# A four-layer graph network on one core: VectorE's order in two attention layers taken from the source, and a layer's second pass cut in two

## The chip, the core and the metric

The kernel runs on one core of a Trainium2 chip. A core has five engines that each work through their own list of instructions: TensorE (PE in the profile; its weight loads are shown as PEld), VectorE (DVE), ScalarE (ACT), GpSimd (POOL) and SyncE (SP), which here only issues loads. An engine takes its instructions strictly in the order of its list, and they wait for each other across engines through semaphores. The metric is the device time of one execution in microseconds.

## What is computed

4096 nodes with 64 features each pass through four layers, each followed by a residual and a layer norm, over one dense 4096 x 4096 matrix of zeros and ones (64 MB in float32, read once per layer from DRAM):

```python
x = _layernorm(x + _L0_gnn_ref(x, adj, L0_gnn_W, L0_gnn_b), axis=-1)       # mean over neighbours, linear, relu
x = _layernorm(x + _L1_gnn_ref(x, adj, L1_gnn_r, L1_gnn_w_att, ...), axis=-1)  # hyperbolic attention
x = _layernorm(x + _L2_gnn_ref(x, adj, L2_gnn_weight, L2_gnn_bias), axis=-1)   # weights 2**-(rank among neighbours)
x = _layernorm(x + _L3_gnn_ref(x, adj, L3_gnn_att_w, ...), axis=-1)        # hyperbolic attention
```

Layers 1 and 3 do the same work: for every pair (i, j) the sigmoid of left[i] + right[j], times the edge, times a distance factor, and the sum over j of that times a vector of node j. Then each node is moved by that sum on the hyperbolic ball, which is a long chain of small formulas with one value per node (norms, reciprocal square roots, a tanh).

## The kernel before

**Tiling.** The receiving nodes are cut into 4 groups of 1024 (`GROUPS` = 3, 2, 1, 0, in that order), the sending nodes into 32 blocks of 128, taken from 31 down to 0, two at a time (a step `g`, 16 steps per group). One load (`load`, L655) brings 128 x 2 x 1024 edges, 1 MB, into one of six buffers.

**Attention (layers 1 and 3).** `attend` does one group. For each of the two blocks `k` of a step, TensorE puts six matmuls of 512 columns into a tile `z` of PSUM (L935, L938, L941; two such tiles exist), ScalarE computes a sigmoid (L943) and a square of z (L946), and VectorE multiplies (L949). After both blocks VectorE combines 2048 columns (L951), and TensorE adds the result into `acc` with four float32 matmuls (L955). So a step holds three large VectorE instructions: L949, L949, L951.

**The rest of a layer** is written as Python generators that are put into two queues and advanced while the large loops are traced: `tick(n)` advances them n times, and a generator says with `yield k` how many ticks to wait before its next piece. `need(tag)` ticks until a piece is done. In a step of attention there are three ticks' places: after each L949 and after the matmuls L955; `rate` ticks at each. The generators that matter here:

- `move` (L966): for a group whose sums are complete, four transposes, a reduce, then the chain of the hyperbolic step: 128x8 instructions (one value per node) on VectorE, six 128x512 ones (L988, L991, L997, L999, L1068, L1071), two products on GpSimd (L992, L1067), a square and a tanh on ScalarE. It holds three `rsqrt` (L669), each a chain of ten 128x8 instructions in which every one reads the one before. Its tiles (u, w_att, k, ...) exist once, so that one group's move can't pass another's.
- `linear` (L1073): the layer 2 linear of a moved group, in halves.
- `norm_rows` (L761) and `prepare` (L782): layer norm, and everything that the next attention needs of a group: 128x8 chains, six 128x512 instructions, casts and four copies on ScalarE, 32 transposes on TensorE, and two logarithms for which ScalarE loads another table.
- `spread_left` (L899): the left values of a group, spread over partitions (L904, L910).

How long a generator waits is set by `soon`, `near` and `after`, which look at `place[0]`, the stage: 0 for layer 0, 1 for layer 1, 2 for layer 2, 3 for layer 3.

**Who sets the order.** The framework's scheduler orders the instructions of each engine by its own estimate of when they can start, unless an engine is named in `tc.manual_schedule(engines=...)`: there it keeps the order in which the source issued them. Before, layers 0 and 2 fix TensorE and ScalarE (`FIXED`); in both attention layers every engine's order is the scheduler's. What came out for VectorE in attention: nearly everywhere one small instruction between two large ones, so three per step.

**Layer 2** makes two passes (L1316 on), each over two groups at once: for each block and group four matmuls into the group's `z` (L1340), an exponential of 1024 columns on ScalarE (L1349) and, one turn later, four matmuls into the group's `acc` (L1356). VectorE only checks every second load (L741, 128x2048). When a pass ends, both its groups go on to `end_2` and then to `norm_rows` and `prepare` of layer 3.

**The tail.** After the last step of layer 3 the last group's `move` remains, and the store of its rows.

Of the kernel before, what the change touches and what calls it, by code (L numbers as in the profile page):

```python
# [19 lines left out]
P = 128  # L20
# [38 lines left out]
def gnn_stack_kernel(  # L59
# [509 lines left out]
    def stream(fits):  # L569

        with ExitStack() as st:
# [46 lines left out]
            def soon():  # L618


                return 0 if place[0] in (0, 2) else 1

            def after(small):


                each = {0: 1.6, 2: 6.0}.get(place[0])
                return 1 if each is None else 1 + int(small / each)
# [41 lines left out]
            def rsqrt(a, name):  # L669

                n = a.shape[1]
                r, t = nums(name, n), nums("rs_t", n)
                V.tensor_scalar(
                    r.bitcast(I32), a.bitcast(I32), -0.5, float(0x5F3759DF), ALU.mult, ALU.add
                )
                for _ in range(3):
                    V.tensor_mul(t, r, r)
                    V.scalar_tensor_tensor(t, t, -0.5, a, ALU.mult, ALU.mult)
                    V.scalar_tensor_tensor(r, t, 1.5, r, ALU.add, ALU.mult)
                return r  # L680
# [64 lines left out]
            def curved(c, name, least):  # L745
# [7 lines left out]
                V.tensor_copy(rsc, rsqrt(c, "rsc"))  # L753
# [7 lines left out]
            def norm_rows(layer, s, v, x2_to):  # L761
# [7 lines left out]
                yield soon()  # L769
                yield soon()  # L770
# [3 lines left out]
                r = rsqrt(m, "n_r")  # L774
# [6 lines left out]
            def prepare(layer, s, att, b_att, curve, least, good, small):  # L781
# [7 lines left out]
                V.reciprocal(rbg, bg)  # L789

# [6 lines left out]
                def second():  # L797
# [16 lines left out]
                    V.tensor_sub(ys[:, :, D : 2 * D], y, ys[:, :, :D])  # L814
# [4 lines left out]
                    yield 1  # L819
                    V.tensor_add(w, xg, over(g))  # L820
                    yield 1
                    V.tensor_mul(xe[:, at, :], w, over(m))

# [3 lines left out]
                    rt = rsqrt(q1, "rt")  # L827
# [34 lines left out]
                    yield 1  # L862
# [109 lines left out]
            def move(layer, s, sums, curve):  # L972
# [14 lines left out]
                yield near()  # L987
# [7 lines left out]
                yield near()  # L995
                yield soon()
# [9 lines left out]
                V.scalar_tensor_tensor(t2, d, -2.0, kx, ALU.mult, ALU.add)  # L1006
                V.tensor_mul(t2, t2, k)
# [7 lines left out]
                V.scalar_tensor_tensor(un, t2, root, rsqrt(t2, "r_t2"), ALU.mult, ALU.mult)  # L1015
# [5 lines left out]
                yield near()  # L1021
# [11 lines left out]
                V.tensor_add(den, den, xy)  # L1033
                V.tensor_sub(p, y2, p)
# [10 lines left out]
                V.scalar_tensor_tensor(w2, qd, 2.0, px, ALU.mult, ALU.add)  # L1045
                V.tensor_mul(t, t, uu)
# [5 lines left out]
                n = rsqrt(t, "n")  # L1052
# [10 lines left out]
                r = rsqrt(w2, "n")  # L1063
# [5 lines left out]
                yield soon()  # L1069
                yield soon()  # L1070
# [3 lines left out]
            def linear(layer, s, weights, finish):  # L1074

                for h in range(2):
# [19 lines left out]
                    finish(slice(s * WB + h * SB, s * WB + (h + 1) * SB), t)  # L1096
# [3 lines left out]
            def supports(at, t):  # L1100

                nc.scalar.activation(halves[:, at, :D], t, AF.Copy, scale=SUP)
                V.scalar_tensor_tensor(
                    halves[:, at, D:], t, SUP, halves[:, at, :D], ALU.mult, ALU.subtract
                )
# [21 lines left out]
            with ExitStack() as lp:  # L1127
# [45 lines left out]
                def own_part(at, t):  # L1173

                    V.tensor_add(xw[:, at, :], t, b0_sb[:, None, :].to_broadcast([P, SB, D]))

                def end_0(s, tops):
# [3 lines left out]
                    for top, low in tops:  # L1181
# [6 lines left out]
                        ts.append(t)  # L1188
                    for h, t in enumerate(ts):
# [6 lines left out]
                    held.clear()  # L1196
                    V.tensor_scalar(z, z, 0.0, None, ALU.max)
                    sq, n2 = grp("sq"), nums("n2")
                    nc.gpsimd.tensor_mul(sq, z, z)
                    yield 1  # L1200
                    V.tensor_reduce(n2, sq, AX.X, ALU.add)
                    V.tensor_scalar(n2, n2, 1e-24, None, ALU.max)
                    n = rsqrt(n2, "n")
# [9 lines left out]
                with tc.manual_schedule(engines=FIXED):  # L1213
                    for s in GROUPS:
# [42 lines left out]
                        if s > 0:  # L1257
                            own_of = linear(0, s - 1, w0_sb[:D, :], own_part)
                            later(in_turn((0, s - 1), own_of))

# [20 lines left out]


            attention(1, curve1, (2, 1, 1, 1), lambda s: linear(2, s, w2_sb, supports))


            place[0] = 2

            def end_2(s, sums):
# [4 lines left out]
                yield 1  # L1293
# [15 lines left out]
            lag = []  # L1309

            def flush():

                while lag:
                    lag.pop(0)()

            with tc.manual_schedule(engines=FIXED):  # L1316
                for n in range(0, NW, 2):
                    two = GROUPS[n : n + 2]
                    zs = [ps.tile([P, WW], F32, name="z") for _ in two]

                    accs = [[] for _ in two]
                    behind = [None, None]
                    for g in reversed(range(NB // 2)):
                        edges = []
                        for s in two:
                            a, edge = load(s, g)
                            if g % 2 == 1:
                                junk = sb.tile([P, 2, WW], F32, name="t").bitcast(BF16)
                                check(s, g, a, junk[:, 0, :].rearrange("p (b i) -> p b i", b=2))
                            edges.append(edge)  # L1330
                        need((2, 2 * g // WB))
                        for k in (1, 0):
                            j = 2 * g + k
                            for i, edge in enumerate(edges):
                                z, acc = zs[i], accs[i]
                                here = edge[:, k * WW : (k + 1) * WW]
                                for lhs, rhs in ((pass_by, behind[i]), (enter, here)):
                                    for h in range(0, WW, W):
                                        if rhs is not None:
                                            nc.tensor.matmul(  # L1340
                                                z[:, h : h + W], lhs, rhs[:, h : h + W],
                                                start=j == BLOCKS[0], stop=True,
                                                skip_group_check=True,
                                            )
                                behind[i] = here
                                flush()

                                w = sb.tile([P, 2, WW], F32, name="sq").bitcast(BF16)[:, 0, :WW]
                                nc.scalar.activation(w, z, AF.Exp, bias=at_edge, scale=-LN2)  # L1349

                                def add(acc=acc, j=j, w=w):
                                    if not acc:
                                        acc.append(ps.tile([P, W], F32, name="acc"))
                                    for part in range(2):
                                        for h in range(2):
                                            nc.tensor.matmul(  # L1356
                                                acc[0][h * D : (h + 1) * D, :],
                                                halves[:, j, part * D : (part + 1) * D],
                                                w[:, h * W : (h + 1) * W],
                                                start=j == BLOCKS[0] and part == 0,  # L1360
                                                stop=j == BLOCKS[-1] and part == 1,
                                            )

# [102 lines left out]
```

## Time and profile before

Three executions took 1150.9 to 1157.15 us, median 1155.24. The profiled one took 1151.7 us, of which its span on the core is 1150.0 us; the other 1.7 us lie around it. By stages, from the trace (busy us of each engine in the stretch, the granted TensorE clock as a share of full speed, and what the DMA queues moved):

| stage | from, to (us) | length | PE | DVE | ACT | clock | GB/s |
|---|---|---|---|---|---|---|---|
| layer 0 | 0 to 192.7 | 192.7 | 167.7 | 147.2 | 38.0 | 0.96 | 386 |
| layer 1, attention | 192.7 to 537.6 | 344.9 | 320.5 | 328.7 | 300.0 | 0.98 | 196 |
| layer 2 | 537.6 to 764.7 | 227.1 | 212.3 | 123.5 | 167.8 | 0.99 | 284 |
| layer 3, attention | 764.7 to 1114.9 | 350.2 | 316.6 | 337.2 | 304.2 | 0.98 | 184 |
| tail | 1114.9 to 1150.0 | 35.1 | 2.9 | 24.2 | 2.2 | 0.58 | 18 |

In lines of a timeline the columns are: start and duration in us, engine, line of the source, operation, tile written <- tiles read, shapes, count, and in brackets the engine's idle time before it and what ended it. [...]what an instruction costs is the distance from its start to the next one's.

### The profile page before, as it was taken

The page shows a single profiled execution, that of the slowest core. Times are in us where ns is not written, and L with a number is a line of the kernel's source. Part 1 is how long each engine was busy: PE and PEld are TensorE (multiplying, and loading weights), DVE is VectorE, ACT ScalarE, POOL GpSimd, SP SyncE. Part 2 cuts the span into 40 slices and gives each one's busy share as a digit, 9 for nine tenths or more (in the row PEclk, how much of TensorE's full clock was granted, in tenths as well). Part 3 has the DMA queues.
Part 4 walks back from the last instruction along what each step waited for, and adds up shares of the span by engine and source line. Part 5 has one row for each costly group of instructions (what it writes and reads, how often), then busy time and mean ns, then how long its engine had stood idle before and what let it go on. Part 6 is the DMA issues. An engine that isn't in the chain of part 4 may idle for free.

```text
span 1150.0 us, 13516 instructions
## 1 busy us (share of the span) xinstructions
PE 1019.8 (89%) x4917; PEld 389.6 (34%) x4917; DVE 960.8 (84%) x1901; ACT 812.2 (71%) x823; POOL 60.9 (5%) x97
## 2 busy tenths in 40 slices
PE   6889997899899999988999997998788999899970
PEld 3445554233333333332333232332323333233220
DVE  7587888989999899989773584249988999999996
ACT  0003215899889799976767688777997999889860
POOL 0020120000000000000000020001100000000001
PEclk9998998999999999999999999999998999999995
DMA  9999898546456455643988886695354655555400
GB/s 352 421 385 412 358 390 337 199 158 217 180 214 220 156 214 215 220 160 141 323 300 310 314 308 255 227 358 193 110 183 155 223 213 215 210 211 212 154 0 22
DMA packets 38418, 271.57 MB, mean 236 GB/s; under 512 B 4550, under 2 KB 4550, under 8 KB 5574
## 3 DMA queue, kind: packets, MB, share of 16 engines
q1 hardware_dynamic: 37440, 269.50, 63.0%
q10 hardware_dynamic: 902, 1.12, 0.3%
q8 instruction: 40, 0.66, 0.2%
q14 instruction: 36, 0.29, 0.1%
HBM read 269.55 MB, written 1.05 MB: 235 GB/s over the span
## 4 chain that ended last, share of the span: by engine, by line
DVE 54%; PE 30%; ACT 6%; DMA 5%; issue 2%; POOL 2%; ACTq 0%; POOLq 0%; SPq 0%; DVEq 0%
DVE t L951 21%; DVE t L949 21%; PE z L1340 9%; PE acc L1356 5%; PE acc L1229 5%; DMA edges<-in_adj_dram 5%; PE acc L955 3%; ACT sq L946 2%; ACT sq L1349 1%; PE aux L1092 1%; PE z L935 1%; PE aux L842 1%; ACT sig L943 1%; PE z L938 1%; DVE junk L741 1%
## 5 line engine op out<-in xcount | busy, mean ns | idle before, releaser
L943 ACT ACTIVATE sig<-left_b,right 128x1024 f32<-128x1024 f32 x256 | 293.8, 1149 | 44.8 <-DVE t L949 33.7
L949 DVE SCALAR_TENSOR_TENSOR t<-z,sig 128x1024 f32<-128x1024 f32 x256 | 309.8, 1215 | 15.5 <-ACT sq L946 14.6
L946 ACT ACTIVATE sq<-z,turn 128x1024 f32<-128x1024 f32 x256 | 281.4, 1105 | 30.2 <-PE z L941 27.9
L951 DVE SCALAR_TENSOR_TENSOR t<-sq,t 128x2048 f32<-128x2048 f32 x128 | 292.9, 2288 | 0.7
L955 PE MATMUL acc<-t,xe 128*64 128x512 f32 x1024 | 260.3, 622 | 33.5 <-DVE t L951 30.0
L935 PE MATMUL z<-edges,two_i 128*128 128x512 bf16 x512 | 202.7, 396 | 20.5 <-DVE t L949 20.3
L941 PE MATMUL z<-dst,src 74*128 74x512 f16 x512 | 196.2, 383 | 0.0
L938 PE MATMUL z<-lo_hi,hi_lo 128*128 128x512 f16 x512 | 195.4, 382 | 0.0
L1349 ACT ACTIVATE sq<-z,at_edge 128x1024 bf16<-128x1024 f32 x128 | 141.8, 1113 | 57.0 <-PE z L1340 56.1
L955 PEld LDWEIGHTS acc<-t,xe 128*64 128x64 f32 x1024 | 64.2, 139 | 171.3 <-DVE t L951 89.3
L741 DVE SCALAR_TENSOR_TENSOR t<-edges 128x2048 bf16<-128x2048 f32 x32 | 73.7, 2312 | 47.1 <-DMA edges<-in_adj_dram 46.2
L1229 PE MATMUL acc<-edges,first 128*128 128x512 bf16 x256 | 82.5, 404 | 19.4 <-DMA edges<-in_adj_dram 19.4
L935 PEld LDWEIGHTS <-two_i 128*128 128x128 bf16 x512 | 50.5, 99 | 141.6 <-issue 97.7
L1356 PE MATMUL acc<-sq,halves 128*64 128x512 bf16 x512 | 80.1, 393 | 16.8 <-ACT sq L1349 16.1
L1229 PE MATMUL acc<-edges,third 128*65 128x512 bf16 x256 | 81.8, 402 | 0.0
L741 DVE SCALAR_TENSOR_TENSOR junk<-edges 128x2048 bf16<-128x2048 f32 x32 | 73.1, 2285 | 7.8 <-DMA edges<-in_adj_dram 7.5
L1340 PE MATMUL z<-edges,enter 128*128 128x512 bf16 x256 | 78.9, 390 | 0.0
L1340 PE MATMUL z<-edges,pass_by 128*128 128x512 bf16 x248 | 77.8, 394 | 0.0
L938 PEld LDWEIGHTS <-hi_lo 128*128 128x128 f16 x512 | 50.5, 99 | 69.4 <-issue 25.8
L941 PEld LDWEIGHTS <-src 74*128 74x128 f16 x512 | 49.6, 97 | 69.3 <-issue 5.1
L1356 PEld LDWEIGHTS <-halves 128*64 128x64 f16 x512 | 19.2, 108 | 73.9 <-issue 73.8
L1229 PEld LDWEIGHTS <-first 128*128 128x128 bf16 x256 | 24.4, 100 | 48.1 <-issue 21.0
(260 smaller groups left out, 758.9 us busy)
## 6 DMA issues: line engine op xcount, KB each, us to landing
edges<-in_adj_dram SPq DMA_DIRECT2D x256, 1024.0 KB, 5.6
x<-in_x_dram SPq DMA_DIRECT2D x4, 256.0 KB
out_dram<-x ACTq DMA_DIRECT2D x4, 256.0 KB, 4.2
w_sb<-in_L_gnn_W_dram ACTq DMA_DIRECT2D x1, 32.0 KB, 4.7
given<-in_L_gnn_b_dram ACTq DMA_DIRECT2D x1, 0.2 KB
given<-in_L_gnn_bias_dram ACTq DMA_DIRECT2D x1, 0.2 KB
given<-in_L_gnn_b_att_dram ACTq DMA_DIRECT2D x1, 0.0 KB
given<-in_L_gnn_att_b_dram ACTq DMA_DIRECT2D x1, 0.0 KB
```

The costliest lines, as they stand in the source:

```text
L741: V.scalar_tensor_tensor(junk, a, 0.0, a, ALU.not_equal, ALU.not_equal, accum_out=odd[:, n : n + 1])
L935: nc.tensor.matmul(half, two_i, edge[:, at : at + W], start=True, stop=False)
L938: nc.tensor.matmul(half, hi_lo[:, of], lo_hi[:, to], start=False, stop=False)
L941: nc.tensor.matmul(half, src[:, of], dst[:, to], start=False, stop=True)
L943: nc.scalar.activation(sig, left_b, AF.Sigmoid, bias=right[:, j : j + 1])
L946: nc.scalar.activation(sq[:, k], zp, AF.Square, bias=turn, scale=-1.0 / UNIT)
L949: V.scalar_tensor_tensor(t[:, k], zp, 0.0, sig, ALU.max, ALU.mult)
L951: V.scalar_tensor_tensor(t, sq, HIGH**2, t, ALU.add, ALU.mult)
L955: nc.tensor.matmul(acc[h * D : (h + 1) * D, :], xe[:, j, :], t[:, k, h * W : (h + 1) * W], start=j == BLOCKS[0], stop=j == BLOCKS[-1],)
L1229: nc.tensor.matmul(accs[h][:m], lhs[:, j, :], edge[:, at : at + W], start=j == BLOCKS[0], stop=j == BLOCKS[-1],)
L1340: nc.tensor.matmul(z[:, h : h + W], lhs, rhs[:, h : h + W], start=j == BLOCKS[0], stop=True, skip_group_check=True,)
L1356: nc.tensor.matmul(acc[0][h * D : (h + 1) * D, :], halves[:, j, part * D : (part + 1) * D], w[:, h * W : (h + 1) * W], start=j == BLOCKS[0 ...
```

## The change

Five things change; in the changed file the lines below L617 move down by 3 to 16, and further in layer 2.

1. Both calls of `attention` stand in `tc.manual_schedule` for VectorE alone; TensorE, ScalarE and GpSimd stay with the scheduler. So VectorE's small instructions stay where the ticks put them: in lumps of 1 to 16 between two large instructions.
2. The generators get other waits: a new `back()` (3 ticks in attention) where another engine's answer is awaited, `yield soon()` inside `rsqrt` and between formulas, so that a chain is cut into lumps of 3 to 6; `after` gives 0 instead of 1 in attention. `rsqrt` becomes a generator with its own temporary.
3. In layer 3 the first group ticks 2 at a time instead of 4.
4. Layer 2's second pass over groups 1 and 0 becomes two passes of one group (`narrow_pass`): first group 1, then group 0. A narrow pass uses the two z tiles for the two halves of 512 columns of its one group, with two exponentials of 512 columns per block instead of one of 1024. Group 1's `end_2`, `norm_rows` and `prepare` are issued during the pass of group 0.
5. Layer 0 ends with `need((0, 0, "sums"))`, and the last ticks run at `place[0] = 4`.

In the built program, a `move` in attention becomes these lumps on VectorE: 2, 1, 1, 1, 4, 4, 4, 3, 6, 10, 3, 6, 5, 4, 3, 4, 11, 3, 5, 1, 1 instructions, spread over some 9 steps that begin 2 to 7 steps after the group's end; the steps after that hold no small instruction until the next group's end. Three moves lie so within each attention layer, the fourth after it. TensorE's order in a step (two z tiles, then the four L955 matmuls of an earlier step) stays.

```diff
             def soon():
                 return 0 if place[0] in (0, 2) else 1
 
+            def back():
+                return near() if place[0] in (0, 2) else 3
+
             def after(small):
                 each = {0: 1.6, 2: 6.0}.get(place[0])
-                return 1 if each is None else 1 + int(small / each)
+                return 0 if each is None else 1 + int(small / each)
...
-                for _ in range(3):
+                for n in range(3):
                     V.tensor_mul(t, r, r)
                     V.scalar_tensor_tensor(t, t, -0.5, a, ALU.mult, ALU.mult)
                     V.scalar_tensor_tensor(r, t, 1.5, r, ALU.add, ALU.mult)
+                    if n < 2:
+                        yield soon()
                 return r
...
                 V.tensor_sub(v, v, over(m))
                 nc.gpsimd.tensor_mul(sq, v, v)
-                yield soon()
-                yield soon()
+                yield back()
                 V.tensor_reduce(v2, sq, AX.X, ALU.add)
...
                 nc.scalar.activation(th, un, AF.Tanh, scale=lam)
-                yield near()
+                yield back()
                 V.scalar_tensor_tensor(un, r_un, fac, th, ALU.mult, ALU.mult)
...
-            attention(1, curve1, (2, 1, 1, 1), lambda s: linear(2, s, w2_sb, supports))
+            with tc.manual_schedule(engines={mybir.EngineType.DVE}):
+                attention(1, curve1, (2, 1, 1, 1), lambda s: linear(2, s, w2_sb, supports))
...
+            def narrow_pass(s):
+                zs = [ps.tile([P, WW], F32, name="z") for _ in range(2)]
+                acc = ps.tile([P, W], F32, name="acc")
+                behind, lag = [None, None], []
+                for g in reversed(range(NB // 2)):
+                    edge = load_2(s, g)
+                    for k in (1, 0):
+                        j = 2 * g + k
+                        w = sb.tile([P, 2, WW], F32, name="sq").bitcast(BF16)[:, 0, :WW]
+                        for h in range(2):
+                            here = edge[:, k * WW + h * W : k * WW + (h + 1) * W]
+                            count(zs[h], behind[h], here, j, W)
+                            behind[h] = here
+                            weights_of(zs[h], W, w[:, h * W : (h + 1) * W])
+                        if lag:
+                            add_up(acc, *lag.pop(0))
+                        lag.append((j, w[:, :W], w[:, W:]))
+                        tick(1)
+                add_up(acc, *lag.pop(0))
+                return [acc]
...
             with tc.manual_schedule(engines=FIXED):
-                for n in range(0, NW, 2):
-                    two = GROUPS[n : n + 2]
...
+                for some in (GROUPS[:2], GROUPS[2:3], GROUPS[3:]):
+                    accs = wide_pass(some) if len(some) == 2 else narrow_pass(some[0])
+                    for s, acc in zip(some, accs):
                         sums = row.tile([P, W], F32, name="sums", bufs=2)
-                        nc.scalar.copy(sums, acc[0])
+                        nc.scalar.copy(sums, acc)
                         later(end_2(s, sums))
...
-            attention(3, curve3, (4, 1, 1, 1), store)
+            with tc.manual_schedule(engines={mybir.EngineType.DVE}):
+                attention(3, curve3, (2, 1, 1, 1), store)
+            place[0] = 4
```

`count`, `weights_of` and `add_up` are the old loop's matmuls, exponential and matmuls as functions. `wide_pass` is the old loop for one pair of groups.

## The prediction

> **What bounds the kernel now.** I read the slices of the page first, then the busy times by stage (the table above), then the timeline of VectorE inside attention, then the tail.
>
> ```profile
> PE   6889997899899999988999997998788999899970
> DVE  7587888989999899989773584249988999999996
> ACT  0003215899889799976767688777997999889860
> ```
>
> In both attention stages VectorE is at nine tenths in nearly every slice and TensorE is close behind; in layer 2 (slices 19 to 26) VectorE is half idle and TensorE sets the pace. The chain of waits agrees: VectorE has 54% of it, 41.7% on the two large attention lines L951 and L949. So what counts in attention is how long one step of VectorE lasts. Two stretches of its timeline, without small instructions and with three:
>
> ```profile
> 264.36 2.29 DVE L951 SCALAR_TENSOR_TENSOR t<-sq,t 128x2048 f32<-128x2048 f32 x1
> 266.57 2.37 DVE L949 SCALAR_TENSOR_TENSOR t<-z,sig 128x1024 f32<-128x1024 f32 x2
> 268.98 2.29 DVE L951 SCALAR_TENSOR_TENSOR t<-sq,t 128x2048 f32<-128x2048 f32 x1
> 271.26 2.55 DVE L949 SCALAR_TENSOR_TENSOR t<-z,sig 128x1024 f32<-128x1024 f32 x2
> 273.84 2.29 DVE L951 SCALAR_TENSOR_TENSOR t<-sq,t 128x2048 f32<-128x2048 f32 x1
> ```
>
> ```profile
> 1098.38 2.29 DVE L951 SCALAR_TENSOR_TENSOR t<-sq,t 128x2048 f32<-128x2048 f32 x1
> 1100.59 0.16 DVE L678 SCALAR_TENSOR_TENSOR rs_t<-rs_t,t 128x8 f32<-128x8 f32 x1
> 1100.66 1.22 DVE L949 SCALAR_TENSOR_TENSOR t<-z,sig 128x1024 f32<-128x1024 f32 x1
> 1101.80 0.15 DVE L679 SCALAR_TENSOR_TENSOR r_t<-rs_t,r_t 128x8 f32<-128x8 f32 x1
> 1101.87 1.22 DVE L949 SCALAR_TENSOR_TENSOR t<-z,sig 128x1024 f32<-128x1024 f32 x1
> 1103.01 0.15 DVE L677 TENSOR_TENSOR rs_t<-r_t 128x8 f32<-128x8 f32 x1
> 1103.12 2.29 DVE L951 SCALAR_TENSOR_TENSOR t<-sq,t 128x2048 f32<-128x2048 f32 x1
> ```
>
> From L951 to L951: without small work 4.62 and 4.86, mean 4.74 us; with three small instructions again 4.74. VectorE itself needs 4.59 for its three large ones (2.21 + 1.14 + 1.24 start to start). The rest without small work is a loop through the others: the end of L951 frees L955 on TensorE (1.87), then both z tiles (2.65), then the square L946 (1.1), and only then the second L949 of the step after next. So a small instruction alone in a gap costs 0.07 to 0.12 us, and three per step are free. The tail shows what they cost one behind the other:
>
> ```profile
> 1126.15 0.69 DVE L1071 TENSOR_TENSOR x<-u,w_att 128x512 f32<-128x512 f32 x1 [0.93 <-POOL w_att L1067]
> 1126.88 0.69 DVE L991 TENSOR_TENSOR u<-z,k 128x512 f32<-128x512 f32 x1
> ...
> 1131.25 0.17 DVE L1008 TENSOR_TENSOR t<-t,uu 128x8 f32<-128x8 f32 x1
> 1131.45 0.17 DVE L1009 TENSOR_SCALAR t<-t 128x8 f32<-128x8 f32 x1
> 1131.66 0.17 DVE L673 TENSOR_SCALAR r_t<-t 128x8 int32<-128x8 int32 x1
> ```
>
> Here each instruction reads the one before, and the distance is 0.20 us; independent neighbours elsewhere in the tail stand 0.08 apart. The first two lines show a second thing: the last group's L991 had its inputs at 1120.4 (L989 at 1120.21), but waited until 1126.88 for the tile u, which group 1's late move held until L1071.
>
> **What the Trainium skill says.** "Perfetto Trace Analysis", section "Optimizing Scalar/DVE Operations", puts the fixed cost of a VectorE instruction at about 60 ns of engine time, with a recorded latency of about twice that because half of it overlaps the next instruction; the trace agrees (0.16 recorded, 0.07 to 0.08 between independent ones). "VectorE: DVE Perf Modes", section "The DRAIN you can't avoid", says that a semaphore between chained instructions costs nothing extra. Here the trace disagrees, 0.20 against 0.08, and I use the trace. "PSUM — Partial Sum Buffer", section "PSUM bank collisions raise a hardware error", has ScalarE and VectorE kept apart on one bank; so L949 follows L946 on the same z, and the trace has it 0.07 to 0.15 after L946's end. "ScalarE: Activation LUTs", section "What ACT_TABLE_LOAD costs", gives 1283 ns; the page of this kernel has the same mean.
>
> **The change part by part,** against the profiled execution's span, 1150.0 us.
>
> *Lumps in attention.* A lump costs the sum of its distances, since after it two z tiles at most are ready and VectorE can't make up more than its slack. One move, by the distances of the tail for the lumps of the built program: six 128x512 instructions at 0.60 (two with a dependent follower) 3.8; the lumps of 4, 4, 4, 3, 6 up to the tanh 0.73 + 0.56 + 0.68 + 0.48 + 1.25 = 3.7; those of 10, 3, 6, 5, 4, 3, 4 after it 1.15 + 0.4 + 0.57 + 0.6 + 0.68 + 0.48 + 0.75 = 4.6; 11, 3, 5 give 1.73 + 0.48 + 0.76 = 3.0. Together 15.1 us; in layer 1 L1103 adds two of 0.34, 15.75. The prepare at the head of layer 3 (group 0 alone): 1.4 + 1.5 + 1.6 + 1.1 + 1.6 + 2.2 + 2.4 + 1.7 + 0.4 + 2.9 = 16.7 by the same distances. At the head of layer 1, with what remains of group 1, 22.7.
>
> Layer 1: 64 steps of 4.59 are 293.8; + 22.7 + 3 x 15.75 = 363.7. Some 30 steps hold no small work and pay the loop's 0.15, + 3.9. TensorE and ScalarE have extra work of their own: the step with left's transposes exceeded 4.74 by 1.65, 3.0 and 1.5 us before (near 296, 885 and 1087 us), and prepare loads two tables; I take 7. Sum 374.7, against 344.9 measured from the first L949 to the last L951: + 29.8. It may start 1.5 earlier, since the first L949 no longer stands behind the normalisation of layer 0 (first L949 at 192.74, its square done at 191.2): + 28.3. Before, only two moves and a start lay in this stage; the other two ran in layer 2 where VectorE is idle, which hid them. After, one of these stays there.
>
> Layer 3: 293.8 + 16.7 + 3 x 15.1 + 3.8 + 7 = 366.6, against 346.8 (768.1 to 1114.9): + 19.8. In this sum is the gain of the split: before, both groups' prepares ran here, the first dozen steps taking 23.6 more than 4.74 each; after, group 1's runs in layer 2. Its cover there is VectorE's idle time (18.0 of 50 us busy from 600 to 650).
>
> Tail: group 1's move ends three steps before the loop does, so L991 of the last group starts at about 1120.5 relative to the same loop end: - 6.4. From there the chain of 0.20 distances stays as it is.
>
> *Layer 2.* Matmul counts stay. The third prepare here adds five sets of transposes and matmuls at 0.45 (2.01 against 1.56 us per turn, 2.3) and one more logarithm between exponentials (a turn of 3.97, + 2.4); one more start of a pass, about 0.9, as between the two passes before. Two exponentials of 512 columns have no row before. From below they cost 2 x 0.53 (half of the 1.06 between two 1024 ones), from above 2 x 0.62 (L994, 128x512): 1.24 at most in a turn of 1.56 that TensorE sets, so I take nothing; without that cover it would be 64 x 0.2 = 13. Copies on ScalarE stall a narrow pass a little more: + 1.4. Sum + 7. The checks (L741) and loads stay as many, at one per 3.1 us.
>
> *Layer 0, rates, the last ticks.* Other waits of a few ticks behind loads that move 386 GB/s: 0. The lower rate in layer 3's first group only spreads its lumps over five steps, within the 16.7; at the tail nothing else is issued that `place[0] = 4` could move.
>
> Sum: 28.3 + 19.8 - 6.4 + 7 = + 48.7 us. The median of the runs stands 3.5 above the profiled time: 1155.2 + 48.7 = 1204, and I say **1205 us**.
>
> **Rivals.**
> *The slack takes more.* No loss in empty steps, no stall of the others (- 22), layer 2 at + 3: 1178. For it: right behind a lump a step took 4.58. Chance 0.15.
> *New waits at the head of VectorE's list.* In a fixed order it can't pass L876 by (lines of the changed file in this paragraph and the last) while TensorE and ScalarE turn a group's rows, or L1085 while GpSimd multiplies, or L1035 while ScalarE takes the tanh; the next L949, and through z TensorE, stand behind it. L999 waited 1.4 us for GpSimd that way. Three such places in eight moves and prepares would add 3 x 8 x 1.4 = 34: 1238. Against it: `back()` puts three ticks, a step of 4.7 us, before each. Chance 0.12.
> *Faster: TensorE is the bound, and the lumps hide behind it.* It is 93% busy in layer 1. Then only the tail, - 6.4, the moved prepare, about - 8, and layer 2's + 7 count: 1148. It decides where a step without small work outlasts VectorE's own 4.59 by more than a lump's share, 15 / 16 = 0.9 us; measured is 0.15. And a step of before with 25 other instructions in it (221.62 to 230.33) took 8.71. Chance 0.05.
>
> **How the numbers follow.** The likeliest case, lumps at nearly full price, has 0.66 and spans 1188 to 1225; the other 0.02 is no change. Half a per cent, 6 us, is about what a measurement here can tell. Slower by more: 0.93; within: 0.02; faster: 0.05. For 8 in 10 I go down to the slack case and up to the middle of the case with waits: 1176 to 1232.
>
> **What would show it.** Right: VectorE's steps in attention of two kinds, 4.6 to 4.9 us without small work and 5.5 to 8 with lumps, nine or ten in a row after each group; 0.20 us inside lumps; attention stages of some 373 and 370 us; L1000 to L1003 of the last group with no wait for u; VectorE busier in the narrow passes. Wrong: lumps whose instructions stand 0.08 apart; a step of 4.74 with a lump in it; VectorE idle before L876, L1035 or L1085; a narrow turn well over 1.56 us.

## The result, and the profile after

The changed kernel takes **1212.43 us** (median of 4, 1211.0 to 1214.42) against 1154.35 (4 runs, 1150.9 to 1157.15) of the kernel before: ratio 1.0506, 95% interval 1.0472 to 1.0539. The profiled execution took 1214.42 us with a span of 1212.2, so the spans differ by 62.2 us and the medians by 58.1. The stages below are cut from the spans, as in the prediction.

The slices of the page after:

```profile
PE   6889896799889988987999988888898798798781
DVE  6687887898999999999463585539998998998995
ACT  0013225889769977875767789887897688687670
```

VectorE is at eight and nine tenths in attention as before; it is the other two that have lost tenths there (7s and 8s where 9s stood). So VectorE still sets the pace where there are lumps, and it does so with more of its own time. In the page's chain of waits its share has fallen, from 54% to 46% (TensorE from 30 to 34%, ScalarE from 6 to 11%): from 1115 to 1150 us, in the lumps of a move, the chain lies almost whole on VectorE, and from 1070 to 1094 us, in steps without small work, it runs round the loop of L963, L967, z and the square. Three of the costliest groups of the page:

```profile
L961 DVE SCALAR_TENSOR_TENSOR t<-z,sig 128x1024 f32<-128x1024 f32 x256 | 308.7, 1218 | 40.7 <-ACT sq L958 38.0
L967 PE MATMUL acc<-t,xe 128*64 128x512 f32 x1024 | 264.3, 639 | 78.6 <-DVE t L963 78.2
L963 DVE SCALAR_TENSOR_TENSOR t<-sq,t 128x2048 f32<-128x2048 f32 x128 | 292.9, 2288 | 2.5
```

The large operations themselves last as long as before (1218 and 2288 ns; 1215 and 2288 before). TensorE waits 78.2 us for L963, against 30.0 before. VectorE's own wait for the square L958 is 38.0 us (14.6 before), of which 10.7 is one wait ahead of layer 3's first L961, which the cut below counts with layer 2.

VectorE's timeline near the end of layer 3, two steps without small work, and then one in which a move's last root is worked off:

```profile
1165.27 2.29 DVE L963 SCALAR_TENSOR_TENSOR t<-sq,t 128x2048 f32<-128x2048 f32 x1
1167.58 2.55 DVE L961 SCALAR_TENSOR_TENSOR t<-z,sig 128x1024 f32<-128x1024 f32 x2
1170.16 2.29 DVE L963 SCALAR_TENSOR_TENSOR t<-sq,t 128x2048 f32<-128x2048 f32 x1
1172.37 2.38 DVE L961 SCALAR_TENSOR_TENSOR t<-z,sig 128x1024 f32<-128x1024 f32 x2
1174.78 2.29 DVE L963 SCALAR_TENSOR_TENSOR t<-sq,t 128x2048 f32<-128x2048 f32 x1
```

```profile
1152.32 0.15 DVE L680 TENSOR_TENSOR n_t<-n 128x8 f32<-128x8 f32 x1
1152.51 0.17 DVE L681 SCALAR_TENSOR_TENSOR n_t<-n_t,w 128x8 f32<-128x8 f32 x1
1152.71 0.17 DVE L682 SCALAR_TENSOR_TENSOR n<-n_t,n 128x8 f32<-128x8 f32 x1
1152.91 0.17 DVE L1079 SCALAR_TENSOR_TENSOR p<-p,n 128x8 f32<-128x8 f32 x1
1152.99 0.16 DVE L1080 TENSOR_TENSOR q<-q,n 128x8 f32<-128x8 f32 x1
1153.07 1.22 DVE L961 SCALAR_TENSOR_TENSOR t<-z,sig 128x1024 f32<-128x1024 f32 x1
1154.21 0.68 DVE L1083 TENSOR_TENSOR u<-u,q 128x512 f32<-128x512 f32 x1
1154.81 2.28 DVE L963 SCALAR_TENSOR_TENSOR t<-sq,t 128x2048 f32<-128x2048 f32 x1
```

From L963 to L963 the empty steps are 4.89 and 4.62 us, the two lengths of before. In the lump the dependent instructions stand 0.19 and 0.20 apart, and L1080, which doesn't read L1079, follows it at 0.08. Ten steps in a row from L963's end to L963's end, from the trace, for the third group's move in layer 3: 4.59, 6.10, 5.65, 6.43, 6.28, 5.95, 6.26, 7.40, 6.30, 5.88, together 60.84 us. In the last of them VectorE also waits 0.72 us for the square.

The tail, VectorE's timeline from the last step's end at 1181.93:

```profile
1188.12 0.69 DVE L1000 TENSOR_REDUCE sum<-z 128x8 f32<-128x512 f32 x1 [6.19 <-ACT z L997]
...
1189.10 0.69 DVE L1003 TENSOR_TENSOR u<-z,k 128x512 f32<-128x512 f32 x1
```

L1003 no longer waits for the tile u: it follows its inputs at 7.17 us after the loop's end, where L991 of before came 11.97 after it.

### The profile page after: what moved, and what is told of

It reads as the page before. It is cut to its first block, busy times and chain, and to the rows that moved or that the text cites. A ratio compares the mean times of both kernels' runs of the same rounds, so it can differ in the third digit from the quotient of the medians.

```text
span 1212.2 us, 13474 instructions
## 1 busy us (share of the span) xinstructions
PE 1026.2 (85%) x4831; PEld 392.0 (32%) x4917; DVE 994.4 (82%) x1901; ACT 818.2 (67%) x887; POOL 75.7 (6%) x97
## 4 chain that ended last, share of the span: by engine, by line
DVE 46%; PE 34%; ACT 11%; DMA 5%; issue 3%; POOL 1%; ACTq 0%; SPq 0%; POOLq 0%; DVEq 0%
DVE t L963 15%; DVE t L961 14%; PE z L1392 8%; PE acc L967 7%; PE acc L1407 5%; DMA edges<-in_adj_dram 4%; ACT sq L958 4%; PE z L950 3%; PE z L947 3%; PE z L953 3%; ACT sig L955 2%; DVE junk L746 2%; PE acc L1247 2%; ACT sq L1401 1%; PE aux L854 1%
## 5 line engine op out<-in xcount | busy, mean ns | idle before, releaser
L955 ACT ACTIVATE sig<-left_b,right 128x1024 f32<-128x1024 f32 x256 | 292.8, 1148 | 95.8 <-DVE t L961 93.8
L961 DVE SCALAR_TENSOR_TENSOR t<-z,sig 128x1024 f32<-128x1024 f32 x256 | 308.7, 1218 | 40.7 <-ACT sq L958 38.0
L967 PE MATMUL acc<-t,xe 128*64 128x512 f32 x1024 | 264.3, 639 | 78.6 <-DVE t L963 78.2
L958 ACT ACTIVATE sq<-z,turn 128x1024 f32<-128x1024 f32 x256 | 281.6, 1108 | 47.8 <-PE z L953 46.4
L963 DVE SCALAR_TENSOR_TENSOR t<-sq,t 128x2048 f32<-128x2048 f32 x128 | 292.9, 2288 | 2.5
L947 PE MATMUL z<-edges,two_i 128*128 128x512 bf16 x464 | 184.0, 397 | 29.4 <-DVE t L961 27.6
L1401 ACT ACTIVATE sq<-z,at_edge 128x512 bf16<-128x512 f32 (+1 forms) x192 | 152.5, 829 | 49.2 <-PE z L1392 46.2
L967 PEld LDWEIGHTS acc<-t,xe 128*64 128x64 f32 x1024 | 64.6, 141 | 214.7 <-DVE t L963 132.4
L1392 PE MATMUL z<-edges,pass_by 128*128 128x512 bf16 x241 | 87.3, 399 | 18.3 <-ACT sq L1401 17.2
L1247 PE MATMUL acc<-edges,first 128*128 128x512 bf16 x241 | 77.3, 397 | 19.6 <-DMA edges<-in_adj_dram 19.1
L1392 PE MATMUL z<-edges,enter 128*128 128x512 bf16 x240 | 84.4, 393 | 1.3 <-DVE t L961 1.2
L1004 POOL TENSOR_TENSOR w_att<-x,u 128x512 f32<-128x512 f32 x8 | 16.0, 1996 | 453.8 <-DVE u L1003 453.8
L1392 PEld LDWEIGHTS <-enter 128*128 128x128 bf16 x256 | 24.8, 98 | 48.0 <-issue 25.7
```

The source lines that it names most:

```text
L947: nc.tensor.matmul(half, two_i, edge[:, at : at + W], start=True, stop=False)
L955: nc.scalar.activation(sig, left_b, AF.Sigmoid, bias=right[:, j : j + 1])
L958: nc.scalar.activation(sq[:, k], zp, AF.Square, bias=turn, scale=-1.0 / UNIT)
L961: V.scalar_tensor_tensor(t[:, k], zp, 0.0, sig, ALU.max, ALU.mult)
L963: V.scalar_tensor_tensor(t, sq, HIGH**2, t, ALU.add, ALU.mult)
L967: nc.tensor.matmul(acc[h * D : (h + 1) * D, :], xe[:, j, :], t[:, k, h * W : (h + 1) * W], start=j == BLOCKS[0], stop=j == BLOCKS[-1],)
```

## The experiments

In all of them the stages are cut in the same way: an attention stage runs from the start of its first large operation on VectorE (L949 before, L961 after; in layer 3 of before that is at 768.1 us) to the end of its last L951 or L963, "start" and layer 2 are what lies ahead of them, and the tail ends with the span. Ratios are to the kernel before on the same chip, with 95% intervals.

| kernel | start | layer 1 | layer 2 | layer 3 | tail | median us | ratio |
|---|---|---|---|---|---|---|---|
| before | 192.7 | 344.9 | 230.5 | 346.8 | 35.1 | 1154.35 | |
| changed | 190.1 | 378.8 | 241.5 | 371.5 | 30.3 | 1212.43 | 1.0506 (1.0472 to 1.0539) |
| split alone | 192.2 | 343.9 | 243.3 | 332.3 | 37.5 | 1152.24 | 1.0012 (0.9989 to 1.0035) |
| order alone | 188.9 | 376.7 | 230.1 | 387.2 | 29.9 | 1215.72 | 1.0565 (1.0516 to 1.0614) |
| fixed in layer 1 only | 187.9 | 377.3 | 243.9 | 328.7 | 37.2 | 1180.46 | 1.0256 (1.0210 to 1.0302) |
| fixed in layer 3 only | 189.4 | 345.4 | 246.6 | 371.7 | 32.0 | 1185.98 | 1.0277 (1.0215 to 1.0340) |
| no fixing | 189.3 | 345.2 | 242.3 | 329.8 | 37.5 | 1147.20 | 0.9958 (0.9942 to 0.9975) |

**The split alone.** Layer 2's loop of the changed kernel in the kernel before.

```diff
-                for n in range(0, NW, 2):
...
+                for some in (GROUPS[:2], GROUPS[2:3], GROUPS[3:]):
+                    accs = wide_pass(some) if len(some) == 2 else narrow_pass(some[0])
```

> The kernel before with layer 2's loop of the changed kernel and nothing else. My theory (the lumps are the loss): layer 2 takes the 10 us more that it took in the changed kernel (240.1 against 230.0 from the first to the last accumulation), layer 3 gives back about half of the 23.6 us that the two prepares cost there (one is now under layer 2): 1152 to 1156. Rival, the split is a loss of its own because the prepare that it moves was hidden by slack in layer 3 anyway: 1164 to 1168.

No difference that can be measured. Layer 2 is 12.8 us longer and layer 3 is 14.5 shorter, since one of the two prepares at its head has moved under layer 2. The rival falls.

**The order alone.** The changed kernel with layer 2's old loop (the diff above, backwards).

> The changed kernel with layer 2's loop of the kernel before. My theory: layer 1 as in the changed kernel (378.8 us), layer 3 longer than there by a second prepare in lumps (18.5 us over six steps), layer 2 back to 230, the early u of the last group kept: 1215 to 1228, above the changed kernel. Rival, the split is the loss: 1190 to 1203.

At the low end of the expected range, and not below the changed kernel. Layer 1 is as in the changed kernel; layer 3 is 15.7 us longer than there, by the second prepare in lumps. So the loss comes with the order and the new waits, not with the split; the next runs tell these two apart.

**Fixed in one layer only, and in none.**

```diff
-            with tc.manual_schedule(engines={mybir.EngineType.DVE}):
+            if True:
                 attention(3, curve3, (2, 1, 1, 1), store)
```

> The changed kernel with VectorE's order left to the scheduler in layer 3's attention, fixed in layer 1's. My theory (the fixed order keeps the small operations in lumps, and each layer pays for its own): layer 1 stays at 379 us, layer 3 falls from 371.5 to about 335 (before's 346.8 less the prepare that moved): 1174 to 1184. Rival, it is the new places of the operations (the longer delays, the yields inside a chain) and not the fixing: 1200 to 1214.

> The changed kernel with VectorE's order left to the scheduler in layer 1's attention, fixed in layer 3's. My theory: layer 3 stays at 371.5 us, layer 1 falls from 378.8 to about 345, its value before: 1174 to 1184. Rival, the new places of the operations cost and not the fixing: 1200 to 1214.

> The changed kernel with VectorE's order left to the scheduler in both attention stages; its new yields and layer 2's split stay. My theory (the fixing, by way of the lumps, is the whole loss): the stages of the runs that fixed only one of them put together, layer 1 345, layer 2 244 to 247, layer 3 329, the tail 37, the start 188: 1141 to 1150. Rival, the new places of the operations cost something of their own: 1158 or more.

Each layer pays for its own fixing: layer 1 377.3 against 345.2, layer 3 371.7 against 329.8, and the layer left free is not touched. The median with layer 3 alone is 2 us above its range, all the others are in theirs. With no fixing at all the new yields and the split make the kernel a little faster than before. The rival, that the new places of the operations cost, falls. Cut into groups of 16 steps, and less 4.74 us for each step, layer 3 costs 18.9, 16.1, 16.5 and 16.7 us in the changed kernel and 12.3, 5.2, 4.7 and 4.2 us with no fixing: a move in lumps costs 11 to 12.5 us more than one that the scheduler places. Layer 3's fixing pays 5 to 7 us back in the tail (32.0 and 30.3 against 37.2 and 37.5), as u comes free in time.

**The chains cut.** Is it the dependence between the instructions of a lump, or only their number? Here the nine refining instructions of each root don't read each other.

```diff
-                r, t = nums(name, n), nums(name + "_t", n)
+                r = nums(name, n)
...
-                    V.tensor_mul(t, r, r)
-                    V.scalar_tensor_tensor(t, t, -0.5, a, ALU.mult, ALU.mult)
-                    V.scalar_tensor_tensor(r, t, 1.5, r, ALU.add, ALU.mult)
+                    V.tensor_mul(nums(f"{name}_x{n}", ...), a, a)
+                    V.scalar_tensor_tensor(nums(f"{name}_y{n}", ...), a, -0.5, a, ...)
+                    V.scalar_tensor_tensor(nums(f"{name}_z{n}", ...), a, 1.5, a, ...)
```

> The changed kernel with the nine instructions of each reciprocal root's three refinements made independent: each reads only the root's argument and writes a tile of its own, and the first guess is used as the result, so the refinement is left out of the values; number, size and place of the instructions stay. My theory (0.20 us between dependent instructions, 0.08 between independent ones): 27 instructions of a move and 9 of a prepare each save about 0.12, 3.2 us in each of the six moves in attention and in the last one, 1.1 in each of the two prepares at a stage's head: 24 to 26 us less, 1183 to 1193. Rival, a lump costs by the number of its instructions or by what it delays behind it, whatever they read: 1207 to 1216.

The total is of no use: 6442.75 us. With the coarser roots the kernel's own test of its assumptions did not hold, and its second, slower path ran after the first. The first path ran whole before it, and its stages can be compared: layer 1 365.0 (378.8 in the changed kernel), layer 3 360.4 (371.5), together 24.9 us less. By my distances it should have been 6 x 3.2 + 2 x 1.1 = 21.4. VectorE's timeline there, at the lump that is shown above of the changed kernel:

```profile
1123.90 0.15 DVE L680 TENSOR_TENSOR n_x<-w 128x8 f32<-128x8 f32 x1
1123.97 0.16 DVE L681 SCALAR_TENSOR_TENSOR n_y<-w 128x8 f32<-128x8 f32 x1
1124.05 0.16 DVE L682 SCALAR_TENSOR_TENSOR n_z<-w 128x8 f32<-128x8 f32 x1
1124.13 0.15 DVE L1079 SCALAR_TENSOR_TENSOR p<-p,n 128x8 f32<-128x8 f32 x1
1124.20 0.16 DVE L1080 TENSOR_TENSOR q<-q,n 128x8 f32<-128x8 f32 x1
```

The same five instructions, now 0.07 to 0.08 apart. The step with three such lumps fell from 7.40 to 6.40 us. The rival would have left both layers as they were. So of the 0.20 us that an instruction of a root costs, some 0.12 is waiting for the result before. Only the roots were cut: the stages stay 20 and 31 us above those with no fixing (345.2 and 329.8), with the other instructions still in lumps, and how much of that is waiting was not measured.

**One at a time, with the order still fixed.** Order fixed in layer 1 only, and there a tick's wait after each VectorE instruction of a move and of a root. In this kernel the rows of group 1 are turned for layer 2 before that group's own move has written them, since the later move takes longer than the queue's delay allows; part of the output is of rows not yet moved (turned at 552.97 us, written at 608.79), while the work stays the same.

```diff
+            def alone():
+                if place[0] == 1:
+                    yield 1
...
                 V.tensor_mul(kx, k, x2g)
+                yield from alone()
                 V.scalar_tensor_tensor(t2, d, -2.0, kx, ALU.mult, ALU.add)
+                yield from alone()
```

> The kernel with the fixed order in layer 1's attention only, but with one small instruction of a move per gap instead of lumps: a tick's wait after every VectorE instruction of a move and inside the reciprocal root, while in layer 1. The order stays fixed by the source. My theory (the lumps are the loss, not the fixing): steps of a move fall from 5.2 to 7.4 us to 4.75 to 4.9, only two moves and a part of the third lie in the stage, and layer 1 takes 345 to 356 us instead of 377: 1147 to 1162 in all. Rival, a fixed order loses by itself because VectorE can't pass a waiting instruction by: layer 1 stays above 368, 1171 to 1184.

Measured: 1184.38 us, 1.0293 (1.0239 to 1.0348), in the rival's range, but not by its mechanism. Layer 1 took **339.7 us** instead of 377.3. A step of its first move:

```profile
405.77 2.29 DVE L970 SCALAR_TENSOR_TENSOR t<-sq,t 128x2048 f32<-128x2048 f32 x1
407.98 0.16 DVE L689 SCALAR_TENSOR_TENSOR n<-n_t,n 128x8 f32<-128x8 f32 x1
408.18 0.23 DVE L1115 TENSOR_SCALAR n<-n,k_rsc 128x8 f32<-128x8 f32 x1
408.32 1.22 DVE L968 SCALAR_TENSOR_TENSOR t<-z,sig 128x1024 f32<-128x1024 f32 x1
409.45 0.16 DVE L1119 TENSOR_TENSOR w<-w,n 128x8 f32<-128x8 f32 x1
409.52 1.22 DVE L968 SCALAR_TENSOR_TENSOR t<-z,sig 128x1024 f32<-128x1024 f32 x1
410.66 0.15 DVE L1121 TENSOR_TENSOR p<-p,n 128x8 f32<-128x8 f32 x1
410.78 2.29 DVE L970 SCALAR_TENSOR_TENSOR t<-sq,t 128x2048 f32<-128x2048 f32 x1
```

Four small instructions in a step of 5.01 us; those with three take 4.74 or 4.75 in most steps, under a fixed order too. But a move needs 30 steps this way and a group has 16, so only one move and a half were done when layer 1 ended, and layer 2 took 285.0 us instead of 243.9. TensorE's timeline in layer 2's first pass shows what it stood still for (the matmuls that turn a group's new rows):

```profile
566.99 1.03 PE L1154 MATMUL aux<-ident,x 128*64 128x128 f32 x4 [8.65 <-DVE x L1143]
...
644.19 1.03 PE L1154 MATMUL aux<-ident,x 128*64 128x128 f32 x4 [17.43 <-DVE x L1143]
```

L1143 is the last instruction of a move. Layer 1 is 37.6 us shorter, and layer 2, where the moves come late, 41.1 longer. Part of the 37.6 is no gain but work that has left the stage. What one at a time is worth is seen on the first move. With the step in which its group ends it costs, over 4.74 us for each step, 7.8 us here (31 steps, 293.41 to 448.12 us), 16.1 in lumps (11 steps, 295.56 to 363.76 in the changed kernel) and 6.8 where the scheduler places it (22 steps, 286.31 to 397.38 with no fixing). So the fixed order by itself costs this move about 1 us, and the lumps some 8 more.

**Only the first move one at a time**, the others in lumps, and each group's rows queued after its own move.

```diff
             def alone():
-                if place[0] == 1:
+                if place[0] == 1 and apart[0]:
                     yield 1
...
+            def moved(layer, s, move_s, then):
+                apart[0] = s == GROUPS[0]
+                yield from move_s
+                apart[0] = False
+                later(in_turn((layer + 1, s), then), True)
```

> VectorE's order fixed in layer 1 only; there the first group's move has one small instruction per gap, the other moves stay in lumps; each group's rows for layer 2 are queued when its own move has ended. Made after the run with all moves of layer 1 one by one: its steps with three small instructions took 4.75 us, but layer 2 took 285 us, since the moves no longer fitted. My theory: the first move costs 4 to 6 us instead of 13.4, half of the third move falls into layer 2, and layer 2 has time for it: layer 1 355 to 362 us, layer 2 243 to 250, 1155 to 1166 in all. Rival, what is taken out of layer 1's lumps comes back in layer 2 whole: layer 2 260 or more, 1172 to 1184 in all.

1174.66 us, 1.0171 (1.0138 to 1.0205): 6 below the kernel with all moves in lumps. The total lies in the rival's range, but layer 2 in neither (254.1), so both expectations missed. The first move's steps are the 4.74 to 5.3 us of the run above. Layer 1 takes 364.1 us, but its last step alone 15.4, as the scheduler has put four of layer 2's checks of 2.29 us ahead of its L963; without these 9 us it would be 355. Layer 2 takes 254.1, with three long turns of 10.0, 8.3 and 3.8 us. So most of what leaves the lumps comes back in layer 2, because the moves then end later (the last two x at 593 and 630 us, 565 and 618 with all in lumps). A fixed order that is as good as the scheduler's over the whole kernel was not found.

**Towards a better kernel.** Two things from the traces of before: u held by the move before it (tail), and two sigmoids of layer 3 that the scheduler puts between layer 2's exponentials, with four table loads.

```diff
-                u, w, sq, of = grp("u"), grp("w_att"), grp("sq"), grp("z0")
+                u, w, sq, of = grp("u", 2), grp("w_att"), grp("sq"), grp("z0")
...
                         later(end_2(s, sums))
+                own = right[:, blocks(GROUPS[0])]
+                nc.scalar.copy(own, own)
```

> The kernel before with two buffers for the tile u and nothing else. My theory on the tail: the last group's subtraction that writes u starts when its inputs are there, 6.4 us earlier, and the chain behind it keeps its length: 1144 to 1148. Rival, the chain then stands behind another tile of one buffer, or behind VectorE's own end of the loop: 1150 to 1155.

> As the run with two buffers for u, and the first two sigmoids of layer 3, which the scheduler puts between layer 2's exponentials at the price of four table loads of 1.28 us, held back until layer 2's last sums are copied (a copy of right onto itself there). Theory: the four turns of layer 2 around them, 8.9 us over 1.56 each, lose 7, and layer 3 starts its first block 2 later: 4 to 6 us below the run with two u alone, 1138 to 1144. Rival, TensorE catches up with the loads' time anyway: no difference.

> The kernel before with layer 2's split, two buffers for u and the two sigmoids held back until layer 2's end. The three parts lie in different stages and should add up: layer 2 235 to 238 instead of 243, layer 3 334, the tail 33: 1136 to 1143, below the run without the split (1145.5). Rival, with the table loads gone the split's own price in layer 2 is larger than what it saves in layer 3: 1145 to 1150.

> The changed kernel without the fixed order, with two buffers for u and the two sigmoids held back. From the stages of the earlier runs: start 188, layer 1 345, layer 2 236, layer 3 331, tail 34: 1132 to 1140. Rival, the new yields spoil the scheduler's order and it stays with the kernel before: 1146 to 1154.

Two u alone: 1150.48 us, 0.9997 (0.9976 to 1.0018), no difference, as the rival has it. VectorE's timeline in that kernel's tail says why:

```profile
1122.70 0.69 DVE L1068 TENSOR_TENSOR u<-u,q 128x512 f32<-128x512 f32 x1
1123.31 0.68 DVE L988 TENSOR_REDUCE sum<-z 128x8 f32<-128x512 f32 x1
1124.32 0.69 DVE L1071 TENSOR_TENSOR x<-u,w_att 128x512 f32<-128x512 f32 x1 [0.34 <-POOL w_att L1067]
```

The scheduler now puts L988, the first operation of the last group's move, behind the other move's chain. The tail became 2.4 us shorter instead of 6.4. With the sigmoids held back as well: 1145.49, 0.9947 (0.9928 to 0.9966), 5.0 below the run with two u, as expected, though above the 1138 to 1144 that took a gain of two u for granted; layer 2 is 6.4 shorter. With the split too: **1143.18, 0.9919 (0.9896 to 0.9941)**, layer 2 234.8 and the tail 32.9. This one beats both kernels. Against the split alone its profiled execution, the fastest of its six, gains 8.5 us in layer 2 and 4.6 in the tail, the medians 9.1; its median is just above what was expected. The last one, on the kernel without fixing, took 1149.67, 0.9954 (0.9934 to 0.9974), in the rival's range: layer 2 stayed at 242.7 (242.3 with no fixing). The turns at its last pass's start fell (7.31, 3.46 and 3.61 us in the changed kernel to 3.55, 2.71 and 2.01), but others grew (against no fixing, 4.29 to 5.42 at the first copies and 4.20 to 4.88 at the last logarithm), and layer 3's first large operation comes 2.3 us later after layer 2's last accumulation, since its sigmoid has been held back. Why the turns grow was not tried.

## Why the prediction was right

**Lumps cost the sum of their distances: right.** A move in layer 3 was to add 15.1 us to the floor of 4.59 per step; the ten steps above are 60.84 - 45.9 = 14.9, of which 0.7 is the wait for the square. In layer 1 the three moves add 14.7, 14.6 and 16.6, 45.9 together, where I had 47.3. That it is the dependence that costs 0.20 and not the instruction was worked out from the tail; the run with the chains cut shows it. It also shows the limit of the sentence in the Trainium skill, "VectorE: DVE Perf Modes", section "The DRAIN you can't avoid", that a semaphore costs nothing extra: that was measured on eight copies of 1.7 us each, and here a small chained instruction starts 0.12 us later than an independent one.

**Prepares at a stage's head: too low.** Layer 3's six steps are 46.97 us, 19.4 over the floor (16.7 predicted), layer 1's seven are 58.03, 25.9 over it (22.7). In both, 3.3 us of it are waits, in one step of 8.45 with three small instructions, where VectorE stands twice for the square, 1.3 and 1.9 us.

**Empty steps pay the loop's 0.15: right.** 4.59 to 4.62 and 4.86 to 4.89 in turn, as before.

**Stalls of the others, 7 per layer: too low.** What remains of the stages after the terms above is 378.8 - 293.8 - 25.9 - 45.9 - 3.9 = 9.3 in layer 1 and 371.5 - 293.8 - 19.4 - 44.7 - 3.8 = 9.8 in layer 3. In layer 3 it is mostly the group's end: three steps of 7.57, 7.73 and 8.09 us, the first two with waits of 0.58 or 0.74 and 2.22 for the square, the third with 2.13 for a matmul of the kernel's own test (L1448). With the heads this makes the stages 4.1 and 4.9 us longer than I had.

**Layer 2, + 7: mis-sized, + 11.0 measured.** That the narrow exponentials cost nothing was right: TensorE's undisturbed turns in a narrow pass are 1.57 us (accumulations from 728.04 to 729.61). The term "copies on ScalarE stall a narrow pass a little more, + 1.4" was the one most too small. The changed kernel's timeline of all engines, in the first narrow pass:

```profile
697.80 1.52 DVE L806 TENSOR_TENSOR y<-x,ym 128x512 f32<-128x512 f32 x1
...
699.36 0.62 ACT L809 CAST ys<-y 128x512 f16<-128x512 f32 x1 [1.93 <-DVE y L806]
...
700.92 1.26 ACT L1401 ACTIVATE sq<-z,at_edge 128x512 bf16<-128x512 f32 x2
...
701.65 0.39 PE L1392 MATMUL z<-edges,pass_by 128*128 128x512 bf16 x1 [3.02 <-ACT sq L1401]
```

ScalarE's order is fixed there, so its three casts stand before the next exponentials and wait for y, which VectorE writes behind a check of 2.28 us; the turn takes 4.75 us, 3.2 over 1.56. In the wide pass of before the turn in which the casts of a prepare ran took 2.33. The casts of the third prepare cost another turn of 2.71, so that these two turns alone add 3.6 us where I had 1.4 for all copies. The extra logarithm was 2.6 (2.4 predicted), and layer 3's first large operation comes 1.5 us later after the last accumulation than before (3.9 against 2.4).

**The tail, - 6.4: - 4.8 measured.** The wait for u went as predicted. But L1003 comes 7.17 us after the loop's end, not 5.6: the last eight accumulating matmuls took 3.68 us instead of 1.94, which is below.

**The rivals.** *The slack takes more* is out: no lumped step hid its lump. *New waits at the head of VectorE's list*: in both attention stages VectorE never stood idle over 0.3 us before L876, L1035 or L1085; three ticks were enough. *TensorE is the bound* is out by the result, and by the chain, which is on VectorE in the lumps. Of the 13.5 us by which the spans' difference exceeds the sum of 48.7, the stages' 4.1 and 4.9, layer 2's 4.0 and the tail's 1.6 are losses, and the earlier start gave 1.1 more than I had taken.

**Slips in the working** that move nothing: L951 and L949 have 41.3% of the chain, not 41.7%; where L949 waits for L946 it starts 0.03 us after its end, not 0.07 or more; 0.15 us in 30 steps would be 4.5, and the 3.9 taken is 26 steps' worth; the ten terms of layer 3's head make 16.8, not 16.7.

What I left unsaid is how the scheduler of before gets most of its small work nearly free. The singles show that one instruction per gap is not enough, as a move then takes 30 steps. In the timeline of before the dependent ones stand alone in their gaps, three a step, and independent ones share a gap (a step with eleven took 5.42 us), so that a move takes 20 steps. Its price lies at a move's start: in layer 1 of before two steps took 13.05 and 12.82 us, with 4.8 and 3.8 us of waiting for ScalarE and GpSimd in them, and behind the head the changed order has no step that long (8.13 us at most).

## What to carry to other kernels

Here a small instruction cost what separated it from the one it reads: in the gap after a large operation 0.07 to 0.12 us, in the chain 0.20; so spread chains over gaps, and fill a gap with independent work. Ask next who waits for the chain's end: spread one by one, the first move cost 8.3 us less than in lumps, but the later ones ran into the next stage, which took 41.1 more. And to learn what a change of several parts cost, cut the runs by stages and switch the parts one by one; here the stages added up within a few microseconds.

## What the runs showed of the hardware

TensorE's clock in the tail was not expected. TensorE's timeline of the changed kernel, and below it that of before, at the last accumulation:

```profile
1177.12 1.94 PE L967 MATMUL acc<-t,xe 128*64 128x512 f32 x8
1181.98 3.68 PE L967 MATMUL acc<-t,xe 128*64 128x512 f32 x8 [2.92 <-DVE t L963]
```

```profile
1110.21 1.94 PE L955 MATMUL acc<-t,xe 128*64 128x512 f32 x8
1114.96 1.94 PE L955 MATMUL acc<-t,xe 128*64 128x512 f32 x8 [2.81 <-DVE t L951]
```

After nearly the same idle time, 2.92 and 2.81 us, the eight matmuls take almost twice as long in the one as in the other; the granted clock from 1182 to 1187 us was 0.50, and 1.00 from 1115 to 1119 us in the kernel before. The length of the idle time does not decide it: with no fixing the same matmuls took longer after the very same 2.81 us, as TensorE's timeline there has it.

```profile
1106.62 3.21 PE L967 MATMUL acc<-t,xe 128*64 128x512 f32 x8 [2.81 <-DVE t L963]
```

The Trainium skill, "TensorE: Matmul & The Clock Gate", section "Part 1: The HAM clock gate", has a clock that falls to half after one idle window of about 3.4 us, and the windows run freely of the kernel. The traces agree with the windows: in each of the fourteen, the clock changes only at times that lie whole multiples of 3.41 us apart, and where these times fall differs from trace to trace. In the changed kernel one window ran from 1177.82 to 1181.24 us; TensorE stood still for 2.17 us of it, and the clock was at half from 1181.24 on. In the kernel before, counted back from the fall of its clock at 1120.35, a window ended at 1113.52, in the middle of the pause, which left 1.43 us of idle time in that window and 1.48 in the next, and the clock stayed. The tails of all fourteen kernels go the same way: the window after which the clock fell held 2.03 to 3.05 us of idle time, the three before it at most 1.93. In the whole traces, after their first 12 us, every window that ran at full clock with more than 1.94 us of idle time in it was followed by half clock, and between 1.2 and 1.94 both happened (the ends of matmuls are modelled, so the bound is rough). So here a window had not to be idle throughout, some 2 us of it were enough, and which of two kernels pays 1.7 us in its tail is a matter of where the pause falls. This was read off the traces; no run moved the pause on purpose.
